# Graph message passing on one core: the turned node table made by its own product, and one-column copies from the second chunk on

## The chip, the core and the metric

The kernel runs on one core of a Trainium2 chip. Time is device time in microseconds (us) from the first to the last instruction of the launch, with what lies around it, on that core; lower is better. The kernel before took 4946.77 us (median of 3 runs, 4945.24 to 4949.85).

## What is computed

There are 12,500 nodes with 48 features each, and 400,000 edges sorted by destination, each with 32 features. Every edge joins the features of its destination and source node and its own, goes through a two-layer network, and is added into its destination:

```python
h = jnp.maximum(_layernorm(x, axis=-1), 0.0)
x_i, x_j = h[dst], h[src]
tmp = jnp.concatenate([x_i, x_j, edge_attr], axis=1)
hid = jax.nn.relu(tmp @ W1 + b1)          # 400000 x 128
msg = hid @ W2 + b2
out = x + jax.ops.segment_sum(msg, dst, num_segments=12500)
```

The first layer can be split: `W1` has 48 rows for the destination, 48 for the source and 32 for the edge. So two node tables of 128 columns are made once: table a (destination part with the bias) and table b (source part). For an edge, the input of the relu is a row of a, a row of b and the edge's own product, added up.

## The kernel before

**Prologue** (`node_tables`). The 98 x 128 padded nodes are normalized in six slices, turned so that features lie on partitions (tiles `ht`), and multiplied by the two blocks of the weight: L174 gives table b and then table a, L181 (DVE) and L183 (ACT) bring the products out of PSUM, L184 writes them to DRAM as `tab_b` and `tab_a`. A block-diagonal weight handles two nodes in one matmul of 256 columns. The main part's first gathers stand behind the end of this part, because its buffers take the prologue's place (L251 is the first of POOL's instructions there).

**Main part** (`windows`). Edges go in tiles of 128, eight tiles to a chunk, 391 chunks. As destinations are sorted, a chunk's destinations lie in a window of 80 nodes. For a chunk `c` the work is spread over iterations `c` to `c+2` of one loop whose order is written by hand (`manual_schedule`), engine by engine:

- `prepare(c)`: SP loads the window's rows of table a (L347), the edge features (L349) and the destinations (L351). POOL gathers source rows of table b from DRAM, one indirect DMA of 128 rows for a tile (L358), into `gb`, which has six buffers, so POOL can be six chunks ahead. DVE makes the one-hot matrix of destinations (L366) and its transpose `hot` (L372).
- `before(c)`: PE multiplies edges and window (L384) into PSUM `pre`. `hidden(c)`: DVE adds the gathered rows (L403), ACT applies the relu (L407, L408). `fold(c)`: PE sums hidden rows into the window (L416, L419). `add(c)`: DVE adds that to the segment sums (L426). Every 12 chunks the segment is multiplied by `W2` (L452, L453), added to x (L454) and stored by SP (L458).

A gather of 128 rows isn't the only way to a tile's source rows. Two others relieve POOL:

- *By columns.* `bt` is table b turned, kept in SBUF with nodes along the free axis. A source's values are one column of 4 bytes on each partition. DVE and ACT copy one column per instruction (L339, its address from a register) into `gt`; when 128 columns are there, PE turns the tile into `pre` (L394) and no gather is needed. The copies for a tile are spread over several chunks: 44 a chunk on DVE, 60 on ACT. `tiles_of` works out in which chunk a tile is full, and the last tile of that chunk is then done this way. Numbers for the addresses are loaded into registers ahead of the copies (L274).
- *By single rows.* SP copies single rows of table b, 12 a chunk, to `gs` (L292), which DVE adds (L405).

Before the change, `bt` doesn't exist when the main part begins. In chunks 0 to 12, SP loads a piece of `tab_b` from DRAM into a buffer of the pool `hid` (L301), PE transposes it (L310) and ACT copies it to `bt` (L311). Columns begin at chunk 14 (`COLS = BUILD + 1`), single rows at chunk 3.

The order of the loop, with the two steps that the change deletes:

```python
if c < NCH:
    prepare(c)
    if c < BUILD:
        part = turn_load(c)
    rows(c, st[c].pop("rows"))
columns(c, 0)
columns(c, 1)
...
if c < BUILD:
    turn(c, *part)
```

Of the kernel before, what the change touches and what calls it, by code (L numbers as in the profile page):

```python
# [8 lines left out]
F32 = mybir.dt.float32  # L9
# [7 lines left out]
P = 128  # L17
N, D, DE, HID, E = 12500, 48, 32, 128, 400000
NR = 98
NPAD = P * NR  # L20
ROWS = 99 * P
NT = E // P
T = 8
CE = T * P
# [21 lines left out]

BUILD = (NPAD + CE - 1) // CE
COLS = BUILD + 1  # L50
ROWS0 = 3
END = NT // T

PARTS = ((True, 0, 27, 1), (True, 27, 17, 28), (False, 44, 28, 48), (False, 72, 32, 76))
PART = sum(n for _, _, n, _ in PARTS)
BASE = 108
RPART = 12

BT0 = 16512


SEG, NEXT, SEG2 = 122, 123, 124
WIDTH = 128
SLOTS = (NCH + 2 + P - 1) // P
MOST = 32

# [15 lines left out]
GNACC = 4  # L82


def node_tables(nc, tc, keep, x, ident, w1, b1, tab_a, tab_b, loads, most, check, rest):

    slices = [(0, 8), (8, 16), (24, 20), (44, 20), (64, 20), (84, 14)]
    ns = len(slices)
# [3 lines left out]
    with ExitStack() as es:  # L92
        node = es.enter_context(tc.tile_pool(name="node", bufs=3))
        ps_t = es.enter_context(tc.tile_pool(name="ps_t", bufs=3, space=PSUM))
        ps_n = es.enter_context(tc.tile_pool(name="ps_n", bufs=3, space=PSUM))
# [5 lines left out]
        wb = keep.tile([2 * D, 2, HID], F32, name="wb")  # L101
# [4 lines left out]
        for j, (r0, rb) in enumerate(slices):  # L106
            t = keep.tile([P, rb, D], F32, name=f"xs{j}")
# [9 lines left out]
        hts = []  # L117
# [47 lines left out]
        def table(j, wt, tv, dve):  # L165
# [17 lines left out]
                    nc.scalar.copy(to, of)  # L183
            nc.sync.dma_start(tv[:, r0 : r0 + rb, :], t)  # L184

        for i in range(ns + 3):
            if i < ns:
                centre(i)
            if 0 <= i - 1 < ns:
                scale(i - 1)  # L190
            if 0 <= i - 2 < ns:
                turn(i - 2)
            if i == ns + 1:
                most()
            if i == ns + 2:
                check()
            if 0 <= i - 3 < ns:
                table(i - 3, wb, tb_v, i >= ns)
        for j in range(ns):
            table(j, wa, ta_v, True)  # L200
        rest()
# [2 lines left out]
def windows(nc, tc, gp, bt, ident, idx, x_t, tab_a, tab_b, dst, edge_t, w1, w2s, b2s, out_t):  # L204
# [3 lines left out]
    with ExitStack() as es:  # L208
# [3 lines left out]
        wp = es.enter_context(tc.tile_pool(name="wp", bufs=3))  # L212
# [71 lines left out]
        def rows(c, nodes):  # L284

            for k, n in enumerate(nodes):
# [6 lines left out]
                    gss[of].bitcast(U8)[e % P : e % P + 1, :],  # L293
                    tab8[bass.ds(n, 4 * HID)].rearrange("(o h) -> o h", o=1),
                )

        def turn_load(i):

            n = min(T, NR - i * T)
            t = wp.tile([P, T, HID], F32, name="hid")  # L300
            nc.sync.dma_start(  # L301
                t[:, :n, :],
                tab_b[i * CE : i * CE + n * P, :].rearrange("(t p) h -> p t h", p=P),
            )
            return n, t

        def turn(i, n, t):
            p_t = ps_p.tile([P, T, HID], F32, name="pre")
            for q in range(n):
                nc.tensor.transpose(p_t[:, q, :], t[:, q, :], ident)  # L310
            nc.scalar.copy(  # L311
                bt[:, i * CE : i * CE + n * P], p_t[:, :n, :].rearrange("h t p -> h (t p)")
            )

        regs = {}

# [143 lines left out]
        with tc.manual_schedule():  # L460
            for c in range(NCH + 2):
                if c < NCH:
                    prepare(c)
                    if c < BUILD:
                        part = turn_load(c)
                    rows(c, st[c].pop("rows"))
                columns(c, 0)
                columns(c, 1)
                if 0 <= c - 1 < NCH:
                    before(c - 1)  # L470
                if 0 <= c - 2 < NCH:
                    fold(c - 2)
                if 0 <= c - 1 < NCH:
                    turned(c - 1)

                g, k = group(c - 2)
                if k == GQ - 3 or c == NCH - 1:
                    segment_load(g)
                if g > 0 and k < L // BLK:
                    segment_sum(g - 1, k, BLK)  # L480
                if g > 0 and k == STORE:
                    segment_store(g - 1, L)
                columns(c, 2)
                if 0 <= c - 1 < NCH:
                    hidden(c - 1)
                load(c, 3)
                columns(c, 3)
                if 0 <= c - 2 < NCH:
                    add(c - 2)
                    if k == GQ - 1:  # L490
                        segment_next(g)
                load(c + 1, 0)
                load(c + 1, 2)
                if c == NCH + 1:
                    segment_sum(g, 0, END_L)
                    segment_store(g, END_L)
                if c < BUILD:
                    turn(c, *part)

                if c < PIECES:  # L500
                    s = slice(c * PIECE, (c + 1) * PIECE)
                    nc.sync.dma_start(out_t[:, s], x_t[:, s])
# [126 lines left out]
def tile_gnn_preln(  # L629
# [56 lines left out]
    with tc.tile_pool(name="keep", bufs=1) as keep, tc.tile_pool(  # L686
        name="ps_c", bufs=1, space=PSUM
    ) as ps_c:

        def loads():  # L690

            nc.sync.dma_start(dsts, dst_cols)
            nc.sync.dma_start(b0f, first_f.rearrange("(o c) -> o c", o=1).to_broadcast([P, NCH]))
            nc.sync.dma_start(far, places)
            nc.sync.dma_start(srci[:, :FIRST], src_cols[:, :FIRST])
            nc.sync.dma_start(last, src_last)
            nc.sync.dma_start(tab_a[NPAD:, :], zrow)

            nc.gpsimd.tensor_scalar_add(b0f, b0f, HALF)
            full = NT // T  # L700
            nc.gpsimd.tensor_tensor(
                rel[:, : full * T].rearrange("p (c t) -> p c t", t=T),
                dsts[:, : full * T].rearrange("p (c t) -> p c t", t=T),
                b0f[:, :full].unsqueeze(2).to_broadcast([P, full, T]), op=ALU.subtract,
            )
            if NT > full * T:
                nc.gpsimd.tensor_tensor(
                    rel[:, full * T :], dsts[:, full * T :],
                    b0f[:, full:].to_broadcast([P, NT - full * T]), op=ALU.subtract,
                )  # L710
            nc.gpsimd.tensor_tensor(dsts, rel, rel, op=ALU.mult)

            nc.gpsimd.tensor_tensor(off[:, :2, :], far[:, 1:3, :], far[:, :2, :], op=ALU.subtract)
            nc.gpsimd.tensor_tensor(off[:, 2, :], off[:, 0, :], off[:, 1, :], op=ALU.add)
            nc.gpsimd.tensor_tensor(off[:, 3, :], off[:, 0, :], far[:, 3, :], op=ALU.add)
            nc.gpsimd.tensor_scalar_add(off, off, -MID)
            nc.gpsimd.tensor_tensor(far, off, off, op=ALU.mult)

            spare = keep.tile([P, D], F32, name="spare")
            nc.gpsimd.indirect_dma_start(  # L720
                out=spare, out_offset=None, in_=x[:, :],
                in_offset=bass.IndirectOffsetOnAxis(ap=srci[:, :1], axis=0),
            )

        def rest():

            nc.sync.dma_start(w2s, w2)
            nc.sync.dma_start(b2s, b2.rearrange("(o d) -> o d", o=1).to_broadcast([P, D]))
            nc.sync.dma_start(srci[:, FIRST:], src_cols[:, FIRST:])

        furthest = keep.tile([P, 1], F32, name="furthest")
        widest = keep.tile([P, 1], F32, name="widest")
        far = keep.tile([P, 4, SLOTS], F32, name="far")
        off = keep.tile([P, 4, SLOTS], F32, name="off")

        def most():
            nc.vector.tensor_reduce(furthest, dsts, AX.X, ALU.max)
            nc.vector.tensor_reduce(
                widest, far.rearrange("p k c -> p (k c)"), AX.X, ALU.max
            )  # L740
            nc.vector.tensor_scalar(furthest, furthest, HALF * HALF, None, op0=ALU.is_gt)
            nc.vector.tensor_scalar(widest, widest, MID * MID, None, op0=ALU.is_gt)
            nc.vector.tensor_tensor(furthest, furthest, widest, op=ALU.max)

        def check():

            p_c = ps_c.tile([1, P], F32, name="p_c")
            nc.tensor.transpose(p_c, furthest, ident)
            out_of = keep.tile([1, 1], F32, name="out_of")
            nc.vector.tensor_reduce(out_of, p_c, AX.X, ALU.max)  # L750
            nc.vector.tensor_scalar(flag, out_of, 0.5, None, op0=ALU.is_gt)

            nc.vector.tensor_scalar_add(wcol, wcol, -HALF)
            nc.vector.tensor_scalar(bw, b0f[:W, :], wcol[:W, :], None, op0=ALU.add)

        dsts = keep.tile([P, NT], F32, name="dsts")
        b0f = keep.tile([P, NCH], F32, name="b0f")
        node_tables(nc, tc, keep, x, ident, w1, b1, tab_a, tab_b, loads, most, check, rest)
    outside = nc.values_load(flag[:1, :1], min_val=0, max_val=1)

    with tc.If(outside == 0) as cmp:
# [75 lines left out]
```

## Time and profile before

| | before |
|---|---|
| median of 3 runs | 4946.77 us |
| profiled execution | 4948.09 us, span 4946.4 us |
| PE / DVE / ACT / POOL busy | 65% / 59% / 58% / 54% of the span |
| mean granted TensorE clock | 0.607 |
| gathers L358 | 2784, 953 ns each |
| one-column copies L339 | 22500 on ACT (189 ns), 16540 on DVE (193 ns) |
| single rows L292 | 4608 |
| mean memory traffic | 74 GB/s |

A line of the page's list of groups reads: line, engine, operation, destination and source with their shapes, count, then busy time, mean time of one, and the idle time before the group's instructions with what ended most of it. "Issue" means that the engine waited for nothing that the profile shows. The mean of a short copy is longer than the distance from one to the next[...]. In the timeline a line is start, length, engine, line, operation, names, and the number of like instructions merged into it.

### The profile page before, as it was taken

How to read it: one execution, taken by the hardware profiler on the slowest of the kernel's cores; microseconds unless marked ns; L12 is line 12 of the kernel's file. 1: busy time of each engine (PE TensorE's matmuls, PEld its weight loads, DVE VectorE, ACT ScalarE, POOL GpSimd, SP SyncE). 2: the span in 40 equal slices, each digit the busy share in tenths (PEclk: the TensorE clock that was granted, in tenths of full speed). 3: DMA queues.
4: the chain of work that ended last, by engine and by line, in shares of the span. 5: the costliest groups of instructions: out<-in, count | busy, mean ns of one | idle time of the engine just before them, and what ended most of it. 6: DMA issues, size and time to landing. Idle time of an engine off the chain costs nothing. (4 is left out here: it accounts for less than half of the span.)

```text
span 4946.4 us, 92158 instructions
## 1 busy us (share of the span) xinstructions
PE 3197.2 (65%) x14504; PEld 2884.0 (58%) x14504; DVE 2942.6 (59%) x18764; ACT 2864.2 (58%) x23270; POOL 2675.9 (54%) x2812
## 2 busy tenths in 40 slices
PE   4565666666666666666666666666666666666666
PEld 3555556555555555656555555655666555555656
DVE  3255666666666666566666666666566666666665
ACT  2146666666566666566656566666566666566665
POOL 5555555555555555555555555555555555555552
PEclk7665655566666565556565666555555665666555
DMA  5422222222222222222222222222222222222221
GB/s 208 111 78 71 70 70 67 68 70 72 70 70 68 67 70 71 70 70 69 66 70 71 70 70 68 67 70 70 70 70 68 68 69 71 70 69 69 70 67 51
DMA packets 214695, 363.63 MB, mean 74 GB/s; under 512 B 70419, under 2 KB 119717, under 8 KB 212805
## 3 DMA queue, kind: packets, MB, share of 16 engines
q0 software_dynamic: 89120, 182.66, 14.4%
q1 hardware_dynamic: 124704, 174.89, 11.8%
q14 instruction: 491, 4.01, 0.3%
q8 instruction: 120, 1.97, 0.2%
q10 hardware_dynamic: 260, 0.10, 0.0%
HBM read 337.91 MB, written 22.07 MB: 73 GB/s over the span
## 5 line engine op out<-in xcount | busy, mean ns | idle before, releaser
L358 POOL DMA_INDIRECT gb<-tab_b,srci x2784 | 2654.2, 953 | 2167.6 <-DVE seg L426 1273.1
L339 ACT COPY gt<-bt 128x4 uint8 x22500 | 2421.0, 189 | 1761.1 <-issue 1734.7
L339 DVE COPY gt<-bt 128x4 uint8 x16540 | 1516.0, 193 | 1464.2 <-issue 1457.9
L416 PE MATMUL p_g<-hot,hid 128*128 128x80 f32 x6250 | 1368.2, 407 | 1557.6 <-ACT hid L408 1446.3
L416 PEld LDWEIGHTS p_g<-hot,hid 128*128 128x128 f32 x6250 | 1291.5, 314 | 1648.2 <-ACT hid L408 1528.5
L384 PEld LDWEIGHTS pre<-rhs,lhs 112*128 112x128 f32 x6250 | 1254.8, 306 | 140.1 <-issue 95.7
L384 PE MATMUL pre<-rhs,lhs 112*128 112x128 f32 x6250 | 1291.4, 393 | 52.1 <-DVE hid L403 38.8
L366 DVE TENSOR_SCALAR_CACHE_REDUCE lhs<-row,bw 80x1024 f32<-80x1024 int16 x391 | 498.1, 1274 | 253.5 <-issue 181.1
L403 DVE TENSOR_TENSOR hid<-pre,gb 128x896 f32<-128x896 f32 (+2 forms) x391 | 429.7, 1099 | 67.5 <-remote 53.8
L408 ACT ACTIVATE hid<-hid 128x896 f32<-128x896 f32 (+1 forms) x391 | 376.1, 962 | 120.4 <-DVE hid L403 91.1
L372 DVE TENSOR_TENSOR hot<-wnum,rel 128x640 f32<-128x640 f32 x391 | 322.0, 823 | 95.7 <-issue 95.7
L394 PE MATMUL pre<-ident,gt 128*128 128x128 f32 x610 | 220.0, 464 | 93.6 <-remote 49.8
L419 PE MATMUL p_g<-ident,deg 80*128 80x80 f32 x782 | 237.4, 405 | 2.7 <-issue 2.7
L394 PEld LDWEIGHTS pre<-ident,gt 128*128 128x128 f32 x610 | 164.0, 328 | 101.3 <-remote 53.6
L419 PEld LDWEIGHTS p_g<-ident,deg 80*128 80x128 f32 x782 | 203.4, 317 | 2.7 <-issue 2.7
L426 DVE TENSOR_TENSOR seg<-seg,p_g 128x160 f32 x391 | 120.9, 309 | 51.3 <-issue 23.4
L452 PE MATMUL p_f<-seg,w2s 128*48 128x512 f32 (+1 forms) x134 | 121.9, 1010 | 0.4 <-DVE seg L426 0.4
L407 ACT ACTIVATE hid<-pre 128x128 f32<-128x128 f32 x305 | 81.9, 268 | 60.8 <-DVE hid L403 51.7
L453 PE MATMUL p_f<-seg,b2s 1*48 1x512 f32 (+1 forms) x134 | 111.2, 924 | 0.0
L453 PEld LDWEIGHTS p_f<-seg,b2s 1*48 1x48 f32 x134 | 14.5, 159 | 102.0 <-issue 102.0
L311 ACT COPY bt<-pre 128x1024 f32<-128x1024 f32 (+1 forms) x13 | 12.4, 957 | 94.7 <-remote 71.5
L454 DVE TENSOR_TENSOR xseg<-xseg,p_f 48x512 f32<-48x512 f32 (+1 forms) x67 | 45.0, 671 | 29.7 <-PE p_f L453 22.5
(65 smaller groups left out, 348.7 us busy)
## 6 DMA issues: line engine op xcount, KB each, us to landing
gs<-tab_b SPq DMA_DIRECT2D x4608, 0.5 KB
row<-in_dst SPq DMA_DIRECT2D x390, 160.0 KB
lhs<-in_edge_t SPq DMA_DIRECT2D x390, 128.0 KB
gb<-tab_b,srci POOLq DMA_INDIRECT x2784
rhs<-tab_a SPq DMA_DIRECT2D x391, 40.0 KB
xseg<-in_x_t SPq DMA_DIRECT2D x33, 192.0 KB
out_x<-xseg SPq DMA_DIRECT2D x33, 192.0 KB
hid<-tab_b SPq DMA_DIRECT2D x12, 512.0 KB
```

The lines of the kernel that those rows point to most:

```text
L339: copy(gts[of].bitcast(U8)[:, 4 * e : 4 * e + 4], bt8[:, bass.ds(at, 4)])
L358: nc.gpsimd.indirect_dma_start(out=gb[:, t, :], out_offset=None, in_=tab_b[:, :], in_offset=bass.IndirectOffsetOnAxis(ap=srci[:, c * T + t ...
L366: nc.vector.tensor_scalar(lhs[:W, : n * P], row[:, : n * P], bw[:, c : c + 1], None, op0=ALU.is_equal, op1=ALU.add, accum_out=deg[:, :1],)
L372: nc.vector.tensor_tensor(hot[:, :n, :], wnum.unsqueeze(1).to_broadcast([P, n, W]), rel[:, c * T : c * T + n].unsqueeze(2).to_broadcast([P ...
L384: nc.tensor.matmul(pre[:, t, :], s["lhs"][:K, t * P : (t + 1) * P], s["rhs"][:K, :], start=True, stop=c not in BYCOLS or t < n - 1,)
L394: nc.tensor.matmul(s["pre"][:, s["n"] - 1, :], gts.pop(c), ident, start=False, stop=True)
L403: nc.vector.tensor_add(h[:, :g, :], pre[:, :g, :], s["gb"][:, :g, :])
L408: nc.scalar.activation(h[:, :m, :], h[:, :m, :], AF.Relu)
L416: nc.tensor.matmul(p_g[:, 0, :], s["h"][:, t, :], s["hot"][:, t, :], start=t == 0, stop=t == n - 1)
L419: nc.tensor.matmul(p_g[:, 1, :], s["deg"], ident[:W, :W], start=True, stop=True)
L452: nc.tensor.matmul(p_f[:, :n], w2s, seg[:, 0, s], start=True, stop=False)
L453: nc.tensor.matmul(p_f[:, :n], b2s[:1, :], seg[:1, 1, s], start=False, stop=True)
```

## The change

`bt` is made in the prologue by a product of its own, straight from the tiles `ht`: for half of the block-diagonal weight at a time, up to four tile columns (512 columns) in one matmul, then one copy out of PSUM to `bt` with a stride of 98 words, on ACT or DVE in turn. It stands after the last part of table b and before table a. The load, transpose and copy of chunks 0 to 12 are deleted. With `bt` there from the start, columns begin at chunk 1 and single rows also at chunk 1. The number of columns a chunk on ACT rises from 60 to 64 (both ACT parts have 32 now), that of single rows on SP from 12 to 16; the number tile is 136 words wide instead of 128.

```diff
-BUILD = (NPAD + CE - 1) // CE
-COLS = BUILD + 1
-ROWS0 = 3
+COLS = 1
+ROWS0 = 1
...
-PARTS = ((True, 0, 27, 1), (True, 27, 17, 28), (False, 44, 28, 48), (False, 72, 32, 76))
+PARTS = ((True, 0, 27, 1), (True, 27, 17, 28), (False, 44, 32, 48), (False, 76, 32, 80))
...
-BASE = 108
-RPART = 12
+BASE = 112
+RPART = 16
...
+        def turned(j):
+
+            r0, rb = slices[j]
+            bt_v = bt.rearrange("h (p r) -> h p r", r=NR)
+            for g in range(0, rb // 2, 4):
+                n = min(4, rb // 2 - g)
+                for k in range(2):
+                    p_n = ps_n.tile([P, 2, 2 * HID], F32, name="p_n")
+                    of = p_n.rearrange("h a b -> h (a b)")[:, : n * P]
+                    nc.tensor.matmul(
+                        of, wb[:, k, :],
+                        hts[j][: 2 * D, g : g + n, :].rearrange("k q p -> k (q p)"),
+                        start=True, stop=True,
+                    )
+                    r = r0 + 2 * g + k
+                    to = bt_v[:, :, r : r + 2 * n - 1 : 2].rearrange("h p q -> h q p")
+                    of = of.rearrange("h (q p) -> h q p", p=P)
+                    if k:
+                        nc.vector.tensor_copy(to, of)
+                    else:
+                        nc.scalar.copy(to, of)
...
+        for j in range(ns):
+            turned(j)
         for j in range(ns):
             table(j, wa, ta_v, True)
...
-        def turn_load(i):
-
-            n = min(T, NR - i * T)
-            t = wp.tile([P, T, HID], F32, name="hid")
-            nc.sync.dma_start(
-                t[:, :n, :],
-                tab_b[i * CE : i * CE + n * P, :].rearrange("(t p) h -> p t h", p=P),
-            )
-            return n, t
-
-        def turn(i, n, t):
-            p_t = ps_p.tile([P, T, HID], F32, name="pre")
-            for q in range(n):
-                nc.tensor.transpose(p_t[:, q, :], t[:, q, :], ident)
-            nc.scalar.copy(
-                bt[:, i * CE : i * CE + n * P], p_t[:, :n, :].rearrange("h t p -> h (t p)")
-            )
...
                     prepare(c)
-                    if c < BUILD:
-                        part = turn_load(c)
                     rows(c, st[c].pop("rows"))
...
-                if c < BUILD:
-                    turn(c, *part)
```

With these numbers `tiles_of` gives 328 tiles by columns (305 before) and 48 by single rows (36 before) of 3125 in all.

More of the change, by code (lines that the diff above doesn't have):

```diff
@@ L44 @@
 U8 = mybir.dt.uint8
-BUILD = (NPAD + CE - 1) // CE
-COLS = BUILD + 1
-ROWS0 = 3
+COLS = 1
+ROWS0 = 1
 END = NT // T
-PARTS = ((True, 0, 27, 1), (True, 27, 17, 28), (False, 44, 28, 48), (False, 72, 32, 76))
+PARTS = ((True, 0, 27, 1), (True, 27, 17, 28), (False, 44, 32, 48), (False, 76, 32, 80))
 PART = sum(n for _, _, n, _ in PARTS)
-BASE = 108
-RPART = 12
+BASE = 112
+RPART = 16
 BT0 = 16512
-SEG, NEXT, SEG2 = 122, 123, 124
-WIDTH = 128
+SEG, NEXT, SEG2 = 130, 131, 132
+WIDTH = 136
 SLOTS = (NCH + 2 + P - 1) // P
@@ L82, with node_tables @@
 GNACC = 4
-def node_tables(nc, tc, keep, x, ident, w1, b1, tab_a, tab_b, loads, most, check, rest):
+def node_tables(nc, tc, keep, bt, x, ident, w1, b1, tab_a, tab_b, loads, most, check, rest):
     slices = [(0, 8), (8, 16), (24, 20), (44, 20), (64, 20), (84, 14)]
@@ L757, in tile_gnn_preln @@
         b0f = keep.tile([P, NCH], F32, name="b0f")
-        node_tables(nc, tc, keep, x, ident, w1, b1, tab_a, tab_b, loads, most, check, rest)
+        node_tables(nc, tc, keep, bt, x, ident, w1, b1, tab_a, tab_b, loads, most, check, rest)
     outside = nc.values_load(flag[:1, :1], min_val=0, max_val=1)
```

## The prediction

> **What bounds the kernel now.** I read the page's busy list first: no engine is over 65% busy, so nothing is bound by plain work. Then the waits (us in total, times, longest):
>
> ```profile
> ACT gt L339 <- issue: 1734.7, 2660, 1.5
> PEld p_g L416 <- ACT hid L408: 1528.5, 334, 10.1
> ...
> DVE gt L339 <- issue: 1457.9, 2213, 1.2
> POOL gb L358 <- DVE seg L426: 1273.1, 337, 11.3
> ```
>
> Two things stand out. PE and POOL wait for ACT and DVE, while ACT and DVE wait for nobody: their idle time lies between one-column copies, each gap at most 1.5 us long, "issue". The timeline of one chunk shows what that is (start, length, instruction):
>
> ```profile
> 2007.00 0.94 POOL L358 DMA_INDIRECT gb<-tab_b,srci  x1 [3.79 <-DVE seg L426]
> ...
> 2008.86 2.67 ACT L339 COPY gt<-bt 128x4 uint8 x27 [0.37 <-issue]
> ...
> 2009.75 1.96 DVE L339 COPY gt<-bt 128x4 uint8 x25
> ...
> 2013.35 0.19 ACT L339 COPY gt<-bt 128x4 uint8 x1 [0.53 <-issue]
> ...
> 2014.05 0.19 ACT L339 COPY gt<-bt 128x4 uint8 x1 [0.51 <-issue]
> ...
> 2014.49 0.95 POOL L358 DMA_INDIRECT gb<-tab_b,srci  x1 [0.30 <-issue]
> ...
> 2016.89 2.58 ACT L339 COPY gt<-bt 128x4 uint8 x26 [0.51 <-issue]
> ...
> 2017.76 1.08 DVE L403 TENSOR_TENSOR hid<-pre,gb 128x896 f32<-128x896 f32 x1
> ...
> 2019.11 0.95 POOL L358 DMA_INDIRECT gb<-tab_b,srci  x1 [3.67 <-DVE hid L405]
> ```
>
> ACT copies 27 columns in 2.67 us (0.10 us each), then one per 0.71 us until 2016.89, then 26 in 2.58 us. DVE, and SP's single rows, crawl over nearly the same stretch, which starts about 4.5 us after POOL's first gather and ends about 1.5 us after its last. Near the end of the span, with no gathers left, the L366 of two chunks start at 4900.00 and 4907.69: 7.7 us with all 104 columns. So gathers slow the other engines, and the loop is: burst of gathers, crawl, DVE's last 11 or so columns, the add L403 that frees gb, next burst. Its period follows the burst (6 gathers from 2069.11, then 8, then 7):
>
> ```profile
> 2069.11 0.95 POOL L358 DMA_INDIRECT gb<-tab_b,srci  x1 [3.63 <-DVE seg L426]
> ...
> 2079.90 0.95 POOL L358 DMA_INDIRECT gb<-tab_b,srci  x1 [3.59 <-DVE seg L426]
> ...
> 2093.44 0.95 POOL L358 DMA_INDIRECT gb<-tab_b,srci  x1 [3.84 <-DVE seg L426]
> ...
> 2105.49 0.95 POOL L358 DMA_INDIRECT gb<-tab_b,srci  x1 [3.58 <-DVE seg L426]
> ```
>
> That is 10.79 us for 6, 13.54 for 8, 12.05 for 7: about 1.3 us for each gather, beside a fixed 3.2 us or so.
>
> [...]
>
> **Part by part.** All sums are against the profiled execution (span 4946.4 us, 4948.09 with what lies around it; the runs' median is 4946.77, so a difference carries over).
>
> *Prologue, added.* 28 matmuls of 512 columns. Table a's 98 of 256 columns took 21.3 us back to back, 0.217 each, so 28 × 0.435 = 12.2 us of PE. The 28 evictions go half to ACT (0.59 us for 128x512) and half to DVE (0.69): 8.3 and 9.7 us, beside PE. They write with a stride of 98 words, which no row of before shows; at twice the price DVE would need 19 us, below the plain price I see no reason. PE runs without a gap into table a, and POOL starts gathering only after that (L251 waited 35.5 us for L183), so it all counts: **+12**, up to +19.
>
> *Start-up, removed.* In chunks 0 to 12 go 13 loads of hid on SP, 98 transposes on PE and 13 ACT copies of 1.0 us. With them goes a wait: L403 of chunk 1 starts at 146.12, 0.05 us after the transposes that free its hid buffer, and SP stood 21.2 us for hid (L301). Late rows cost DVE 42.8 us here. *Start-up, added:* columns from chunk 1 and 16 rows from chunk 1. POOL's opening run is six chunks, 48 gathers; chunks 2 to 5 now have a tile by columns each, so it is 8 + 8 + 4 × 7 = 44, 5 us shorter. During that run all engines nearly stand (DVE idle 35 us before L403 at 124.30). DVE's 44 columns of chunk 1 now stand before this L403: at some 0.4 us each for the half that is not done by the standstill, +10. I get L403 of chunk 0 at 124.3 + 12 − 5 + 10 = 141, of chunk 1 at 150, then twelve loops of 12.15: chunk 13 at 296. In the trace of before L366 of chunk 15, right after that add, is at 302. Prologue and start-up together: **−5**. Why so little: chunks 5 to 15 took 12.3 us each with 8 gathers and no columns, and 7 gathers with columns take 12.15. Bounds: if the columns cost nothing in the opening run and SP's late rows vanish, −45; if the evictions are slow and chunk 1's ACT columns too hold the loop, +25.
>
> *Gathers.* Tiles by columns 305 → 328, by rows 36 → 48, so gathers 2784 → 2749. Ten fall into chunks 0 to 13, counted above; the other 25 × 1.3 = **−33**. Lower bound of the price: the last burst of 5 against none (9.13 to 7.7 us) gives 0.3 each, −8.
>
> *Row tiles.* 12 more adds L405 on DVE at 0.28, all in the loop: **+3**.
>
> *ACT, 60 → 64 columns (DVE stays at 44).* 4 × 0.095 = 0.38 us between the crawl's end and the relu. Is there room? After the relu, ACT's next copies need registers loaded behind it, and they start 2.1 us after DVE's add ends whether the relu was early or late: 2006.73 → 2008.86, 4710.74 → 4712.87, 4722.87 → 4725.00. The relu itself (L407 with L408) takes 1.1 and starts 0.3 to 0.65 after the add, so up to about 0.8 nothing moves. With 0.5 + 0.38 it is 0.09 too late; 0.0625 fewer gathers a chunk give 0.07 back. I take 0.03 × 376 chunks = **+11**. Behind ACT's late columns stand PE's L394 and then L403; without this cover the 0.38 costs up to 0.27 a chunk (rival one). Below zero there is nothing to gain.
>
> *SP, 12 → 16 rows.* By the queue waits of SP between 500 and 4500 us it stood 521 us at the store L458 and 35 at L347, 1.7 us a chunk. A row takes 0.34 us outside the crawl and 0.72 on average in a chunk of slow ones (8.64 us for 12). The crawl has its own length, so the four more should fall outside it: 1.4 us, plus a longer register load. It fits with almost nothing left, **0**; SP then runs closely ahead of DVE instead of two chunks, and row loads (L351) queue behind the singles. The 23 more L394 matmul pairs on PE are covered: it waits 1446 us for ACT over the span.
>
> Sum: −5 − 33 + 3 + 11 = −24: span 4922, and 4923 beside the median.
>
> **Rivals.**
> *ACT becomes the bound (slower).* For: it waits for the add only 37.6 us over chunks past 400 us, and its relu follows its copies at once. A chunk with the relu as late as it may be took 12.03 us; plus 0.38 is 12.41 against 12.14 for a burst of 7. Against: the 2.1 us above. From 0.09 us of overflow on, it adds up until L394 holds L403. 0.27 × 376 = +102, fewer gathers at the shorter −27, start −5: 5016.
> *SP becomes the bound (slower).* It decides once four rows cost more than 1.7 us. At 0.53 each (between 0.34 and 0.72) they cost 2.1: 0.4 × 376 = +150, L366 waiting for row in every chunk: 5073. For: the start-up, where SP was already late. Against: its idle time at L458.
> *The start-up pays.* The hid wait and the 42.8 us for row go, the columns hide in the standstill: −45 − 33 + 14: 4882.
> *Nothing moves.* The prologue eats the start-up's gain and a gather is worth 0.6: −5 − 15 + 14, about 4941.
> *The work isn't moved as said:* excluded, L311 and its loads are deleted.
>
> **How the numbers follow.** Differences within 0.2% (±10 us) can't be told from none. My case 0.45 (0.40 of it below 4937), the start-up 0.12, nothing moves 0.12, ACT 0.20, SP 0.11. Faster 0.52, same 0.17, slower 0.31. My case's own range with its unknown prices is 4895 to 4950. To leave out no more than 2 in 10 I reach down to 4870 and up to 5040, which takes in ACT's case and part of SP's. The forecast is 4923.
>
> **What would show it.** Right: 2749 gathers; gathers start near 79 us instead of 67; bursts of 7 still 12.1 to 12.2 us apart; ACT's relu some 0.9 us after the add; SP's wait at L458 nearly gone. Wrong: L394 or L403 waiting for ACT's columns in a third of the chunks (ACT), DVE L366 waiting for row in the steady part (SP), the turned evictions over 1 us each (prologue), or chunk 15 far from 297 us (start-up).

## The result, and the profile after

The changed kernel takes **4989.45 us** (median of 4 runs, 4975.14 to 4991.81) against 4946.76 for the one before: ratio 1.0079, 95% interval 1.006 to 1.0099. It is 0.8% slower; the forecast was 4923, faster. The profiled execution took 4991.18 us, its span is 4989.5, 43.1 more than before.

The waits of the changed kernel (engine, line waited at, what it waited for; us in total, times, longest), to be laid beside those of before:

```profile
ACT gt L344 <- issue: 1699.4, 2554, 5.1
PEld p_g L421 <- ACT hid L413: 1614.2, 355, 36.8
...
DVE gt L344 <- issue: 1396.1, 2145, 1.9
POOL gb L363 <- DVE seg L431: 1287.8, 331, 5.9
...
DVE lhs L371 <- DMA row<-in_dst: 201.7, 49, 6.6
...
DVE lhs L371 <- DMA gs<-tab_b: 126.8, 199, 4.3
```

The crawl (the slowing of ACT, DVE and SP while POOL gathers: from 643.60 ACT copies 32 columns in 3.25 us, from 649.50 to 651.63 one every 0.7 us) is still there, and its lines hardly moved. New is the fifth of these: DVE's one-hot L371 waits 201.7 us for the destinations `row`, in 49 chunks. (The one-hot reads no `gs`, so what the last line stands for isn't shown.) The line of before, and then SP's own queue, first of the kernel before and then of the changed one:

```profile
DVE lhs L366 <- DMA row<-in_dst: 42.8, 11, 6.5
```

```profile
SPq L458 <- DVE xseg L454: 617.7, 33, 30.0
SPq L347 <- PE pre L384: 56.5, 35, 8.8
SPq L292 <- DMA gs<-tab_b: 52.1, 91, 1.4
```

```profile
SPq L463 <- DVE xseg L459: 38.2, 2, 33.0
SPq L315 <- DMA gs<-tab_b: 32.7, 52, 1.4
SPq L352 <- PE pre L389: 22.3, 4, 11.2
```

SP had stood 617.7 us at the store, which means that it was far ahead of DVE and had to let it come up. Now it stands there twice, 38.2 us in all. SP has become an engine with next to no idle time, and it carries `row`, which DVE needs first in each chunk. The timeline of two chunks shows it (start, length, instruction, idle time before it and what ended that; `x16` is 16 row DMAs merged):

```profile
641.78 0.94 POOL L363 DMA_INDIRECT gb<-tab_b,srci  x1 [4.28 <-DVE seg L431]
...
644.04 0.42 SPq L356 DMA_DIRECT2D row<-in_dst  x1
...
644.56 9.24 SPq L315 DMA_DIRECT2D gs<-tab_b  x16
...
647.32 1.28 DVE L371 TENSOR_SCALAR_CACHE_REDUCE lhs<-row,bw 80x1024 f32<-80x1024 int16 x1 [5.58 <-DMA row<-in_dst]
...
654.67 0.94 POOL L363 DMA_INDIRECT gb<-tab_b,srci  x1 [4.45 <-DVE seg L431]
...
656.43 0.41 SPq L356 DMA_DIRECT2D row<-in_dst  x1
...
656.93 10.21 SPq L315 DMA_DIRECT2D gs<-tab_b  x16
...
659.77 1.27 DVE L371 TENSOR_SCALAR_CACHE_REDUCE lhs<-row,bw 80x1024 f32<-80x1024 int16 x1 [5.14 <-DMA row<-in_dst]
```

`row` is issued at 644.04 and DVE uses it at 647.32, 3.3 us later; behind it SP spends 9.24 us on 16 rows before it can issue the next `row`. DVE, which has been free for 5.58 us, sets the chunk's start by SP.

The prologue is the second place. Groups between 46 and 92 us of the changed kernel (busy us, mean ns of a record, idle before):

```profile
L194 PE MATMUL p_n<-ht,wb 96*128 96x512 f32 (+2 forms) x54 | 21.7, 549 | 0.5 <-DVE bt L203 0.5
L173 PE MATMUL p_n<-wa,ht 97*128 97x256 f32 x98 | 21.4, 380 | 0.0
...
L205 ACT COPY bt<-p_n 128x512 f32<-128x512 f32 (+2 forms) x14 | 14.0, 997 | 9.0 <-PE p_n L194 9.0
L203 DVE COPY bt<-p_n 128x512 f32<-128x512 f32 (+2 forms) x14 | 13.7, 997 | 9.6 <-PE p_n L194 9.6
```

The code issues 28 products at L194 and 49 at L173 (one for two of the 98 node columns). The trace has 56 records of the first in all, 54 of them in this window, and 98 of the second: each product stands twice. So 98 records are 49 instructions, a product of 256 columns costs 21.4 / 49 = 0.44 us and the new part as much as the whole of table a. The first gather comes at 90.5 us instead of 67.2, **+23.2** where +12 was forecast.

Where the 43 us come from is seen from the start of each chunk's L371, changed kernel less the one before:

| chunk | 0 | 6 | 16 | 22 | 34 | 46 | 58 | 106 to 358 | 382 |
|---|---|---|---|---|---|---|---|---|---|
| later by, us | 23.3 | 13.0 | 24.4 | 25.6 | 30.7 | 36.6 | 39.1 | 35 to 43 | 38.7 |

The start-up wins 10 us back by chunk 6; then 26 us are lost up to chunk 58; from there on both take 12.34 us a chunk, although the changed kernel has some 20 gathers fewer in that part.

### The profile page after: what moved, and what is told of

Read it like the earlier page. It is cut to its first block, busy times and chain, and to the rows that moved or that the text cites. A ratio compares the mean times of both kernels' runs of the same rounds, so it can differ in the third digit from the quotient of the medians.

```text
span 4989.5 us, 98405 instructions
## 1 busy us (share of the span) xinstructions
PE 3235.6 (65%) x14508; PEld 2907.7 (58%) x14508; DVE 2989.0 (60%) x19366; ACT 3087.8 (62%) x25662; POOL 2638.1 (53%) x2777
## 5 line engine op out<-in xcount | busy, mean ns | idle before, releaser
L363 POOL DMA_INDIRECT gb<-tab_b,srci x2749 | 2616.4, 952 | 2220.7 <-DVE seg L431 1287.8
L344 ACT COPY gt<-bt 128x4 uint8 x24868 | 2644.3, 189 | 1730.4 <-issue 1699.4
L344 DVE COPY gt<-bt 128x4 uint8 x17116 | 1553.5, 190 | 1401.4 <-issue 1396.1
L371 DVE TENSOR_SCALAR_CACHE_REDUCE lhs<-row,bw 80x1024 f32<-80x1024 int16 x391 | 498.1, 1274 | 425.3 <-DMA row<-in_dst 201.7
L413 ACT ACTIVATE hid<-hid 128x896 f32<-128x896 f32 (+1 forms) x391 | 373.3, 955 | 74.8 <-issue 54.1
L399 PE MATMUL pre<-ident,gt 128*128 128x128 f32 x656 | 234.6, 461 | 98.8 <-remote 91.7
L399 PEld LDWEIGHTS pre<-ident,gt 128*128 128x128 f32 x656 | 175.2, 326 | 105.8 <-remote 97.6
L447 DVE MEMSET seg<- 128x944 f32 x64 | 54.1, 845 | 9.3
```

The source lines that it names most:

```text
L344: copy(gts[of].bitcast(U8)[:, 4 * e : 4 * e + 4], bt8[:, bass.ds(at, 4)])
L363: nc.gpsimd.indirect_dma_start(out=gb[:, t, :], out_offset=None, in_=tab_b[:, :], in_offset=bass.IndirectOffsetOnAxis(ap=srci[:, c * T + t ...
L371: nc.vector.tensor_scalar(lhs[:W, : n * P], row[:, : n * P], bw[:, c : c + 1], None, op0=ALU.is_equal, op1=ALU.add, accum_out=deg[:, :1],)
L399: nc.tensor.matmul(s["pre"][:, s["n"] - 1, :], gts.pop(c), ident, start=False, stop=True)
L413: nc.scalar.activation(h[:, :m, :], h[:, :m, :], AF.Relu)
```

## Experiments

Two theories. **SP**: the 16 rows leave SP no slack, so `row` comes late and the saved gathers bring nothing. **ACT**: the 64 columns on ACT end too late and take the gain back. Each run is timed against the kernel before on its own chip, and that turned out to matter: on three chips the kernel before takes 3577 to 3579 us, on two others 4948 and 5003. Times are compared within a chip alone.

### First chip (before: 3577.54 us)

**rows12**: the change, but 12 rows.

```diff
-RPART = 16
+RPART = 12
```

> The changed kernel with 12 single rows a chunk on SP instead of 16; 64 columns on ACT as in the change. Gathers 2761 by the counting rule (12 more than the change). Theory SP (16 rows use up SP's slack, L371 then waits for its destination rows and takes back what the fewer gathers give): SP waits at the store again for some 500 us, DVE's wait for row at L371 falls below 100 us, and the time is 28 us lower for the freed loop plus 16 us for 12 gathers: 4977. Theory ACT (64 columns hold the loop): SP's slack comes back but nothing else moves, 4989 + 16 = 5005. Both the bound at once: near 4990 to 5000.

Measured 3571.88 us, ratio 0.9986 (0.9979 to 0.9992): slightly faster than before.

**act60**: the change, but 60 columns on ACT, with 16 rows.

```diff
-PARTS = (..., (False, 44, 32, 48), (False, 76, 32, 80))
+PARTS = (..., (False, 44, 28, 48), (False, 72, 32, 80))
```

> The changed kernel with 60 columns a chunk on ACT instead of 64; 16 single rows as in the change. Gathers 2761. Theory ACT: the relu starts 0.4 us sooner after the add, as before the change, and the loop gets 28 us back less 16 for 12 more gathers: 4977. Theory SP: the waits for row at L371 stay at 200 us and more, and 12 more gathers cost 16: 5005.

Measured 3588.78 us, 1.0037 (1.0023 to 1.0051).

**both6012**: both edits.

> The changed kernel with 60 columns on ACT and 12 rows on SP, the numbers of before, but columns and rows still from chunk 1 and the turned product in the prologue. Gathers 2773. From chunk 58 on it has as many gathers as before the change (2360), so there its time a chunk must be that of before, 12.34 us, by either theory. If only the start differs, the difference at chunk 58 is the whole of it: prologue +23, start-up about -10: 4960. If the loss between chunks 6 and 58 that the change showed (+26 us) has nothing to do with 64 and 16, it is 4986.

Measured 3587.07 us, 1.0027 (1.0016 to 1.0039).

**before6416**: the kernel before with 64 columns and 16 rows, turned from DRAM as it was.

> The kernel before with 64 columns and 16 rows, everything else (turning in chunks 0 to 12, columns from 14, rows from 3) as before. Gathers 2760, 24 fewer than before. If fewer gathers pay 1.3 us each: 4915. If ACT's or SP's load takes that back, as the time a chunk of the changed kernel says: 4947, with L366 waiting for row and no wait of SP at the store. If the loads alone cost more than they give while SP has no lead at the start: up to 4975.

Measured 3592.2 us, 1.0034 (1.0021 to 1.0046). With 24 gathers fewer and no new prologue it is slower than before, so the new sizes alone can do harm.

The changed kernel itself didn't run on this chip, but rows12 and act60 can be set side by side: both have 2761 gathers, and the one with 16 rows is 16.9 us slower. both6012 has 12 gathers more than rows12 and is 15.2 us slower, which is what those gathers cost (1.25 us each, below). So here the 16 rows cost time and the 64 columns don't. But this chip showed no crawl, so it is not the case that was first measured. The timeline of rows12 on another chip of this kind, from its repeat rows12_2:

```profile
1999.89 0.94 POOL L363 DMA_INDIRECT gb<-tab_b,srci  x1 [0.30 <-issue]
...
2001.14 0.95 POOL L363 DMA_INDIRECT gb<-tab_b,srci  x1 [0.30 <-issue]
...
2001.72 3.14 ACT L344 COPY gt<-bt 128x4 uint8 x32
2002.39 0.94 POOL L363 DMA_INDIRECT gb<-tab_b,srci  x1 [0.30 <-issue]
...
2005.84 3.15 ACT L344 COPY gt<-bt 128x4 uint8 x32 [0.97 <-issue]
```

ACT runs 32 columns in a row while POOL gathers, and POOL issues a gather every 1.25 us, chunk after chunk: 7.06 gathers x 1.25 = 8.83 us, which is the chunk period in that trace. There POOL itself is the bound, if nothing else is late.

### Second chip (before: 3577.28 us)

**again**: the changed kernel, unedited.

> The changed kernel itself, a second time, on whatever chip these runs get. On the chip of the last four runs the kernel before took 3577.5 us. Theory A (there each gather costs POOL 1.25 us and the prologue costs 23.4 us, and four more rows on SP cost 17 us as act60 against its own sum shows, 45 as before6416 does): 35 fewer gathers give -44, so 3577.5 - 44 + 23.4 + 17 to 45 = 3574 to 3602. Rival B (SP's rows cost nothing in themselves, ACT's columns did it): 3557. If these runs land on a chip where the kernel before takes about 4947 us, the changed one should be 0.6 to 1.0% slower again, near 4985.

Measured 3599.39 us, 1.0056 (1.0042 to 1.007). Its waits show what its loop waits for on this chip:

```profile
DVE lhs L371 <- DMA row<-in_dst: 483.7, 267, 9.3
ACT gt L344 <- issue: 379.8, 487, 1.8
```

DVE waits for `row` in 267 of 391 chunks; in rows12_2, beside it, in 2. The second line was 1699.4 us with the crawl, where the change was first measured, and is 379.8 here, with the same code.

**rows12_2**: rows12 beside it.

> rows12 again, beside the changed kernel on one chip: the two differ in the 12 against 16 rows alone, 12 more gathers here. Theory A (SP has no room for four more rows): this one faster than the changed kernel, by 2 to 30 us on the chip of 3577 us, and by 20 us or more on a chip of 4947 us, where SP's lead over DVE was 7.5 us. Rival B (the rows are free, the gathers count): slower than the changed kernel by 12 x 1.25 = 15 us.

Measured 3573.82 us, 0.9992 (0.9984 to 1.0): 25.6 us less than the changed kernel, with 12 gathers more.

**prolog**: the new prologue and nothing turned from DRAM, but columns from chunk 14, rows from chunk 3, and the old sizes; the 2784 gathers of before.

```diff
-COLS = 1
-ROWS0 = 1
+COLS = 14
+ROWS0 = 3
-RPART = 16
+RPART = 12
```

(and the line of act60)

> The turned product in the prologue and nothing turned from DRAM any more, all else as before: columns from chunk 14, rows from chunk 3, 60 columns on ACT, 12 rows; 2784 gathers. It prices the prologue against the removed loads and transposes alone. Theory A (the prologue adds 23.4 us that nothing hides, and the turning lay beside the gathers of the first chunks): 23 us slower than before, 0.4 to 0.7% by the chip. Rival C (the removed turning gives back what the trace of the changed kernel gained by chunk 6, 10 us): 13 us slower. Rival D (it gives it all back): within 5 us of before.

Measured 3599.62 us, 1.0065 (1.0051 to 1.0078): +22.3 us. That is about the prologue in full, so the deleted turning gives next to nothing back here. Against rows12_2, which has 23 gathers fewer, it is 25.8 us slower, 1.1 us a gather.

**pet12**: rows12, with the turned table from transposes of table b's tiles in SBUF, each slice right behind its part of table b.

```diff
-nc.tensor.matmul(of, wb[:, k, :], hts[j][: 2 * D, g : g + n, :]...)
+for q in range(n):
+    nc.tensor.transpose(p_v[:, q, :], t[:, g + q, :], ident)
```

> As rows12 (64 columns on ACT, 12 rows), but the turned table comes from 98 transposes of table b's tiles in SBUF, taken in the prologue behind each slice, in place of the 28 matmuls of 512 columns. Theory A (TensorE's time in the prologue is what counts): 98 transposes of 128 columns against 24.4 us of matmuls, by the 0.11 us a record and the two records of a 128x96 turn some 11 to 22 us, partly in gaps that TensorE has there: first gather between 72 and 86 us instead of 90.5, the time 5 to 18 us under rows12. Rival E (the strided copies out of PSUM, 1.1 us each, then hold the prologue): no gain over rows12.

Measured 3566.25 us, 0.9969 (0.9959 to 0.9979): 7.6 us under rows12_2, inside the range given. But the first gather comes at 86.7 us, only 3.7 earlier than in rows12_2, outside the 72 to 86 expected. The rest of the 7.6 isn't explained. Groups of pet12 between 30 and 90 us:

```profile
L203 ACT COPY bt<-p_n 128x512 f32<-128x512 f32 x13 | 13.8, 1155 | 1.2 <-PE p_n L198 1.2
L198 PE MATMUL p_n<-ident,tab 128*128 128x128 f32 x90 | 12.7, 286 | 1.8 <-ACT bt L203 1.5 <-DVE bt L201 0.2
```

PE's part fell to 12.7 us, but ACT now waits only 1.2 us between its strided copies of 1.155 us each: they have become part of the bound, as rival E (in the expectation above) had it. A turn of 128x96, which the expectation counted as two records, has one in the trace (49 records in the changed kernel for the 49 that the code issues).

### Third chip (before: 5003.15 us, with the crawl)

**here**: the kernel before, with a trace.

> The kernel before, with a trace, on the chip where these runs go. If the crawl of ACT, DVE and SP during the gathers belongs to the chip and not to the kernel (theory A), its trace shows none here: POOL's gathers back to back every 1.25 us, 7.12 of them a chunk, so 8.9 us a chunk, first gather at 67.2, and SP waiting at its store L458. If it is the columns and rows of the changed kernel that removed it (rival), the before still crawls here with bursts of gathers and pauses of 3.6 us.

Measured 5006.99 us. It fell on a crawling chip, so it shows nothing of the other kind; bursts of 7 gathers are 12.27 us apart here (median of 266), 12.15 in the first trace. It does serve as the kernel before for the next run.

**four**: the changed kernel with 13 row DMAs in place of 16, the last bringing four neighbouring rows, so that three of 16 rows are not those asked for.

```diff
+if k == 12:
+    nc.sync.dma_start(gss[of]...[e % P : e % P + 4, :], tab8[bass.ds(n, 16 * HID)]...)
+if k >= 12:
+    continue
```

> The changed kernel with 13 row DMAs a chunk instead of 16: the last one brings four neighbouring rows at once (so a quarter of the rows are not the ones asked for; bytes, tiles, columns and 2749 gathers stay). Theory A (SP's time to issue single rows is the bound): three issues of 0.345 us less are 1.0 us of SP a chunk, DVE's waits for row go from 440 us to under 100, the steady chunk takes 7.03 gathers x 1.25 = 8.79 us, and the time is 3555 to 3565, 35 to 45 us under the changed kernel's 3599. Rival F (the small row transfers, or the 48 tiles by rows with their adds, cost it): 3590 to 3600, as before the edit.

Measured 5009.06 us, 1.0015 (1.0007 to 1.0024). The numbers expected were for the other kind of chip. Against the changed kernel's 1.0079 it is better, but on another chip. SP stands 184.8 us at its store again, and `row` is no longer waited for (0.6 us in all). Its L371 is later than that of `here` by 3.6 us at chunk 6 and 5.5 at chunk 58, where the changed kernel went from 13.0 to 39.1 against its own before. The tiles by rows, the adds, the gathers and the 64 columns are those of the change, so the loss between chunks 6 and 58 comes with the three issues and their transfers. From chunk 58 to 382 `four` gains 9.3 us with 19 gathers fewer, only 0.5 us a gather.

**pet14**: pet12 with 14 rows.

> pet12 with 14 single rows a chunk instead of 12: 2755 gathers against 2761. Theory A (SP stood some 1.4 us a chunk with 12 rows and none with 16, so 14 leave it 0.7; POOL stays the bound): 6 x 1.25 = 7.5 us under pet12, near 3559. Rival G (SP's long chunks, the ones with a store or a segment's load, take up the 0.7 already): at or above pet12's 3566.

Measured 4979.22 us, 0.9951 (0.9937 to 0.9964): faster than before by 24 us. pet12 itself didn't run on this chip, so 14 against 12 rows stays open.

### Fourth chip (before: 3579.34 us)

**again3**, **four_2**, **rows12_3**, **act60_2**: the changed kernel and three of the edits side by side.

> The changed kernel once more, as the reference for the three beside it. On a crawling chip (before near 4950 to 5000 us): 0.6 to 1.0% over before, as at first. On a chip without the crawl (3577 us): 0.4 to 0.7% over, as in the second batch.

> 13 row DMAs a chunk for the same 16 rows' bytes, now beside the changed kernel. SP theory: 30 to 45 us under the changed kernel on either chip. ACT theory (64 columns hold it): within 10 us of the changed kernel on a crawling chip; on one without the crawl still the SP theory's 35 to 45 us, since there DVE's waits for row are seen in the trace.

> 12 rows, 64 columns, 12 gathers more. On a crawling chip, SP theory: SP's lead back over 15 us, the start-up loss between chunks 6 and 58 (26 us) gone, 12 gathers x 1.3 = 16 us given back in part: 10 to 40 us under the changed kernel. ACT theory: as slow as the changed kernel or slower, by up to 16 us. Without the crawl: 26 us under, as measured.

> 60 columns on ACT, 16 rows, 12 gathers more. On a crawling chip, SP theory: SP still has no lead (under 10 us), no faster than the changed kernel, up to 16 us slower. ACT theory: ACT's relu comes again 0.7 us after DVE's add instead of 1.1, and it is 20 us or more faster. Without the crawl: some 10 us under the changed kernel, as the first batch had it (3588.8 against 3599.4).

| run | us | ratio to before | DVE L371 waits for row |
|---|---|---|---|
| again3 | 3581.87 | 1.0005 (0.9995 to 1.0016) | 398.7 us, 222 times |
| four_2 | 3558.70 | 0.9946 (0.9926 to 0.9966) | 49.4 us, 43 times |
| rows12_3 | 3574.21 | 0.9986 (0.9979 to 0.9992) | 9.6 us, once |
| act60_2 | 3573.85 | 0.9986 (0.9979 to 0.9993) | 548.8 us, 293 times |

Three DMA issues a chunk fewer, with the same tiles and gathers, bring 23 us. What differs is SP's issues and their transfers alone, though 23 is under the 30 to 45 expected: again3 was less slow than the changed kernel on the second chip. rows12_3 has 12 gathers more than four_2 and is 15.5 us slower: with SP relieved, a gather is worth 1.3 us here. act60_2 was 8 us under again3, as expected, but it doesn't show a cost of the columns in the loop: between chunks 22 and 382 the two traces have the same pace, 8.84 us a chunk, and nearly all of the difference comes past chunk 382. act60_2 is also as fast as rows12_3, which has the same 2761 gathers: the 16.9 us between these two edits on the first chip aren't seen here, and why is open. The kernels with 16 rows vary more from chip to chip (act60: 1.0037, 0.9986) than those with 12 (rows12: 0.9986, 0.9992, 0.9986).

### Fifth chip (before: 4947.63 us, as in the first measurement)

**again4**, **rows12_4**, **act60_4**: the three that decide, where the crawl is.

> The changed kernel as the reference for the two beside it: 0.6 to 1.0% over before on a crawling chip, 0 to 0.6% over without the crawl.

> 12 rows, 64 columns. On a crawling chip, SP theory: 10 to 40 us under the changed kernel, SP's lead over 15 us. ACT theory: not under it, up to 16 us over. Without the crawl: 8 to 26 us under.

> 16 rows, 60 columns. On a crawling chip, SP theory: within 10 us of the changed kernel or up to 16 us slower, SP's lead still under 10 us. ACT theory: 20 us or more under it, ACT's relu 0.7 us after the add. Without the crawl: 8 to 10 us under.

| run | us | ratio to before |
|---|---|---|
| again4 | 4987.35 | 1.0108 (1.005 to 1.0166) |
| rows12_4 | 4949.67 | 1.0005 (0.9996 to 1.0013) |
| act60_4 | 4997.56 | 1.0094 (1.0077 to 1.0111) |

Four rows fewer on SP take 38 us away, with 12 gathers more. Four columns fewer on ACT take nothing away. SP's waits in again4 and then in rows12_4:

```profile
SPq L463 <- DVE xseg L459: 39.2, 2, 33.9
SPq L352 <- PE pre L389: 25.9, 5, 11.5
```

```profile
SPq L463 <- DVE xseg L459: 575.9, 34, 33.9
SPq L352 <- PE pre L389: 116.7, 58, 11.3
```

With 12 rows SP has its idle time back. Two chunks of rows12_4, for comparison with those of the changed kernel above:

```profile
614.34 0.94 POOL L363 DMA_INDIRECT gb<-tab_b,srci  x1 [3.70 <-DVE seg L431]
...
614.82 1.27 DVE L371 TENSOR_SCALAR_CACHE_REDUCE lhs<-row,bw 80x1024 f32<-80x1024 int16 x1 [0.52 <-issue]
...
615.53 0.41 SPq L356 DMA_DIRECT2D row<-in_dst  x1
...
616.03 7.65 SPq L315 DMA_DIRECT2D gs<-tab_b  x12
...
625.61 1.27 DVE L371 TENSOR_SCALAR_CACHE_REDUCE lhs<-row,bw 80x1024 f32<-80x1024 int16 x1 [0.48 <-issue]
```

L371 starts 0.5 us after POOL's first gather here, in the changed kernel 5.1 to 5.5 us after it, and the `row` issued at 615.53 is for a later chunk. Worked out over the traces by stretches of chunks (time from one `row` issue to its L371 as SP's lead, median; 16 or 12 rows' time on SP, mean; chunk period):

| chunks | again4: lead, rows, period | rows12_4: lead, rows, period |
|---|---|---|
| 6 to 20 | 3.0, 9.4, 12.80 | 16.8, 7.4, 12.49 |
| 20 to 40 | 3.0, 9.5, 12.91 | 19.1, 7.0, 12.24 |
| 40 to 58 | 2.9, 8.8, 12.66 | 21.5, 7.5, 12.37 |
| 200 to 380 | 8.2, 7.8, 12.34 | 21.5, 7.3, 12.31 |

A late SP gets slower: with a lead of 3 us its 16 rows take 9.4 us, with 8 us they take 7.8. More of the late ones fall on the crawl: in the first trace of the changed kernel, where the lead is 3.0 us in chunks 20 to 40 and 7.8 in chunks 200 to 380, 6.1 of the 15 distances from one row of a chunk to the next are over 0.55 us in the first stretch and 3.6 in the second (the others have a median of 0.32). That goes with the loss between chunks 6 and 58: at chunk 58 again4 is 27.6 us behind rows12_4, at chunk 382 36.5. act60_4 stays late longer (lead 3.1 and rows 9.5 still in chunks 40 to 58), though ACT has less to do. What lets SP get away, near chunk 58 in one and later in the other, isn't known.

## Why the prediction was wrong

**The profile of before** was read rightly: crawl, late columns, add, next burst. With SP's rows at 12, bursts of 7 are 12.18 us apart (median, rows12_4) against 12.15 before.

**The failed step: SP, 12 to 16 rows, "0".** The prediction let four rows cost 1.4 us of 1.7 us of slack, and said that SP would then run closely ahead of DVE. It did, and that was the loss. In again4 SP has no idle time worth the name and a cycle of 12.36 us; in rows12_4 it is 12.31 us with about 1.6 of it waiting. So four rows cost 12.36 − 10.7, or 1.7 us, just the slack, and 2.2 while SP is late (12.9 − 10.7). In time, undoing them is worth 38 us with 12 gathers given up (1 us each, see below), so some 50 of the 67 us between forecast and result. Two things were missed. The cost was put outside the crawl, "the crawl has its own length, so the four more should fall outside it", while more of the rows issued late fall inside it (6.1 distances over 0.55 us a chunk against 3.6, see the experiments). And slack that is just used up leaves nothing to make a delay good: SP comes out of the start-up with 3 us of lead and doesn't get away from there for some 50 chunks. The kernel before came out of its own start-up no better (about 3 us in chunks 5 to 17), but with 12 rows it had 16 by chunk 20. In the steady part a smaller loss remains: past 900 us bursts of 7 gathers are 12.35 us apart (mean) in again4 and 12.24 in rows12_4. It goes with the 16 rows, but that SP's time makes it isn't shown: in `four`, which hardly waits for `row`, they are 12.47 apart against 12.32 in `here`. Why the saved gathers bring so little there stays open. The rival "SP becomes the bound" had the mechanism and the sign. It was too large (5073) because it put 2.1 us less 1.7 on every chunk; so much was lost only to about chunk 58.

**Prologue, +12: mis-sized, 23.2.** The 98 records of table a were taken for 98 products. (L416 of the kernel before has 16 records in 3.70 us for the eight products of a chunk, 0.46 us each.) The new part has 98 x 128 columns in its products of up to 512, table a 49 x 256: the same number, and they took 21.7 (54 of 56 records) and 21.4 us. The count in the code (`range(rb // 2)`) would have said so. The strided copies were given the plain price, as the author saw no reason for another and no trace of before has such a copy. Most took 1.12 us, against 0.59 for the plain copy on ACT and 0.69 on DVE; why isn't shown. Behind the slower PE they were hidden: ACT waited 9.0 us for it before its 14 copies, DVE 9.6.

**Start-up, −17 beside the prologue.** Part of it came, and more where SP keeps up: in rows12_4 the delay falls from 24.7 us at the first gather to 10.0 at chunk 6. In the changed kernel L371 of chunk 15 is at 325.2 us, not at 297: 11 us of the 28 are the prologue's, some 8 are SP's, as rows12_4 has 318.3 with a first gather 1.4 us later; the other 9 or so are the start-up's own, forecast too early.

**Gathers, −33.** The count is right, 2749. With 12 rows they were worth some 1 us each rather than 1.3: rows12_4 gains 10.8 us between chunks 22 and 382, where 4 more columns of 128 a chunk save some 11 gathers. In `four` it was 0.5, on the chips without the crawl 1.1 to 1.3.

**ACT, +11.** Too high, as far as it can be told: rows12_4 runs with 64 columns at a chunk period of 12.32 us between chunks 58 and 382 against 12.34 before, and if the 11 gathers that it saves between chunks 22 and 382 were worth the full 1.3 each, the columns cost some 4 us. (The prediction's own 0.09 less 0.07 makes 8, not 11.) ACT's relu L413 did move, from 0.7 us behind the add to 1.0 in again4 and 1.15 in rows12_4 (medians), more than forecast. In act60_4 it is back at 0.56, and nothing was gained. **Row adds, +3** were not measured by themselves.

With the prologue at 23.2 and ACT at 0, the prediction's sum would have been −24 + 11.2 − 11 = −24: still faster. rows12_4, where the SP step is undone, ends at +2.0; the gathers at 1 us and the 12 that it doesn't save account for most of that. So the sign was lost at SP, though rows12_4 itself only comes level with before.

## What to carry to other kernels

An engine that only feeds others needs a lead and not just idle time on the average: when a change fills its slack, look whether its own instructions get dearer where they then fall. Before a duration per record is used, set the number of records beside the number of instructions in the code. Undoing each size of a change alone is cheap and finds the best of both: the new start with 12 or 14 rows and the table turned on PE from SBUF beat the kernel before (0.9969 for pet12, 0.9951 for pet14, on different chips), and pet12 also the changed one beside it.

## What the runs showed of the hardware

- The crawl is a matter of where the kernel runs. On three chips with the kernel before at 3577 to 3579 us and a granted clock of 0.69 to 0.73 in the traces it is absent; on the others, with 0.60 to 0.61, it is there. ACT's idle time before its one-column copies that waits for nothing is 344.0 us in rows12, 379.8 in again and 362.2 in rows12_3, against 1662.8 in rows12_4 and 1713.4 in `four`. The crawl's cause isn't known. On either kind the first gather of the changed kernel comes between 90 and 93 us (90.5 in its first trace and 91.9 in rows12_4 with the crawl, 90.4 in rows12_2 without), so the difference is in the gathering part.
- A single-row DMA costs SP 0.34 us to issue without the crawl (12 in 4.07 and 4.15 us in rows12). Where the crawl is, 16 take 7.8 to 9.5 us in the means above, depending on where in the burst they fall: in chunks 30, 31 and 40 of again4 those outside it mostly start 0.32 to 0.4 us apart, those inside 0.7 to 1.4.
- A copy of 128x512 from PSUM to SBUF with a stride of 98 words took 1.12 us on ACT and DVE in the changed kernel (1.16 on ACT in pet12), against 0.59 for the plain one on ACT and 0.69 on DVE.
